# A two-layer cross-attention kernel: layer 2's weight splitting moved into layer 1, with the split tiles kept in DRAM

## The chip, the cores and the metric

The kernel runs on one core of a Trainium2 chip. The metric is the device time of one execution in microseconds (us), the median of the runs listed. Engines are named as the profile does: PE (TensorE), ACT (ScalarE), DVE (VectorE), POOL (GpSimd), and SP (SyncE), whose instruction queue issues nearly all DMAs here.

## What is computed

Two cross-attention layers run one after the other on the same 16 batches of 256 queries (320 channels, 20 heads of 16). The context has 256 rows of 512 numbers. Layer 1 takes 77 rows of it as text and 179 as image tokens, layer 2 takes 252 and 4. Cut to what matters:

```python
def layer(x, ctx, mask, Wq, Wk, Wv, Wk_ip, Wv_ip, Wout, bout):
    text, ip = split(ctx)                       # 77 | 179 rows in layer 1, 252 | 4 in layer 2
    q = x @ Wq; k = text @ Wk; v = text @ Wv
    probs = softmax(q_h @ k_h.T / 4)            # per head
    out = probs @ v_h
    sem = ...                                   # from the text probabilities and the raw context
    ip_probs = softmax(q_h @ (ip @ Wk_ip)_h.T / 4 + 0.5 * sem) * mask
    out = out + ip_probs @ (ip @ Wv_ip)_h
    return out @ Wout + bout + x
```

Everything is float32. The kernel multiplies in a rounded format and keeps accuracy by splitting each operand into a high part and a low part (the remainder) and adding three products.

## The kernel before, in words

Work goes in slots. Layer 1 has 80 (16 batches x 5 groups of four heads, `NS = 80`), layer 2 another 80. `slot0` and `slot1` write the attention of a slot by hand: scores (L744), their maxima (L745, L746 on DVE), the turned scores (L768), exponentials (L771 on ACT), the multiplication by the image factor (L774 on POOL), and the values (L801 on PE), which end in `settle0`. Everything else, such as keys, queries, contexts and the output projection of a finished batch, is a task: a generator with a list of due times in slots. `fill(now)` steps each task whose time has come, between the pieces of a slot. The PE order is exactly the order in which the code is written. On the other engines a scheduler places the instructions, unless `queued` ties one behind the last anchor (the last score maximum, exponential or multiplication) of its engine. Each engine then works through its own list strictly in order, SP's list of DMAs included.

The keys and queries of a slot are loaded by SP four slots ahead (`stacks0`, `LEAD = 4`) into a ring of four tiles each, `ks` and `qs`. Their transfers are `ks<-kd`, `qs<-qd`, `ks<-M` and `qs<-tph`.

The output of a batch b of layer 1 goes through `finish`: `gather` transposes the heads' results (`hT`, L831 on DVE), `split` makes the operand `ho` (L282 on ACT, L283 and L284 on DVE), and `project` multiplies it with `wF` (L609 for two thirds of the rows, L612 for the last). For odd batches the split is due at slot 5b+6 and the first L609 group at 5b+7.2.

Layer 2's weights are prepared late in layer 1 by the tasks `w7` (image keys, then `wA`), `w6` (values `wC`, image values), `w2` (queries `wE`), and in the first slots of layer 2 by `("w4", 1)` (output `wF`). All use `in_turn` and `halves`: a DMA brings a 128-row piece into one of two `rawc` buffers, ACT copies it rounded (L164), and DVE and POOL subtract to get the low part (L167, in three pieces for the weights in heads' layout). Two also multiply a part by a mask (L218). The tiles `wA`, `wC`, `wE` and `wF` hold layer 1's weights until layer 1 is done with them, and `wB` is a ring of four.

Of the kernel before, what the change touches and what calls it, by code (L numbers as in the profile page):

```python
# [8 lines left out]
F32 = mybir.dt.float32  # L9
# [7 lines left out]
B = 16  # L17
S = 256
H = 20
# [31 lines left out]
def xattn2(  # L51
# [129 lines left out]
    def columns(s, m):  # L181

        at = m * 128 if not s else CH + 64 + m * 128
        return slice(at, at + 128)

    def rows(w, k):

        return w[k * 128 : (k + 1) * 128]

    def in_turn(parts, wait, tag="raw", eng=nc.vector, later=False):  # L190

        ahead, parts, tags = [], list(parts), tag.split()
        for i in range(len(parts) + 1):
            if len(tags) > 1:
                new = () if i else range(len(parts))
            else:
                new = range(i + 1 if i else 0, min(i + 2, len(parts)))
            if i:
                halves(*ahead.pop(0), eng, wait)
            for j in new:  # L200
                src, hi, lo = parts[j]
                raw = buf(tags[j // 2 % len(tags)], [128, 512], bufs=2)
                shape = src.shape
                raw = raw[:, : shape[1]] if len(shape) == 2 else raw.rearrange("p (k n) -> p k n", k=shape[1])
# [13 lines left out]
            nc.vector.tensor_scalar_mul(w[:, 2, CH : 2 * CH], f(w[:, 2, CH : 2 * CH]), half)  # L218
        return lambda s, k, m: w[:, k, columns(s, m)]

    def weights_by_column(w_d, wait=0, raw="raw"):

        parts = [buf("wB", [128, 2, 4, 128], FR, bufs=SIZES["WB"]) for m in range(3)]
        src = w_d.rearrange("(k p) n -> p k n", p=128)
        yield from in_turn([(src[:, :, m * 128 : (m + 1) * 128], w[:, 0], w[:, 1]) for m, w in enumerate(parts)], wait, raw)
        return lambda s, k, m: parts[m.start // 128][:, s, k]

    def weights_by_row(w_d, wait=0, raw="raw"):

        parts = [buf("wB", [128, 2 * CH + 4], FR, bufs=SIZES["WB"]) for k in range(4)]  # L230
        yield from in_turn([(rows(w_d, k), *rounded(w)) for k, w in enumerate(parts)], wait, raw)
        return lambda s, k, m: parts[k][:, columns(s, m)]

    def prod(out, lhs, rhs, kt):

# [240 lines left out]

    def weights7():
        cip = w1["cip"]
        wki1 = yield from weights_by_row(wki1_d, 0.3, "rawc")
        for m in range(3):  # L480
            kp = prod_m(bank()[:, :BI], wki1, m, lambda s, k: cip[:, s, k], 4)
            evacuate(kip[:, 0, m], kip[:, 1, m], kp, m)
            yield
        w1["k"] = yield from weights(wk1_d, "wA", None, 0.3, "rawc")

    def weights6():
        cip = w1["cip"]
        wv = w1["wv"] = buf("wC", [128, 2, 4, H * D + NIP], FR)
        parts = [(wv1_d[k * 128 : (k + 1) * 128], wv[:, 0, k, : H * D], wv[:, 1, k, : H * D]) for k in range(4)]
        yield from in_turn(parts, 0.3, "rawc")  # L490
        wvi1 = yield from weights_by_column(wvi1_d, 0.3, "rawc")
        vip = buf("rawc", [128, 512], bufs=2, name="vip")[:BI, :CP]
        for m in range(3):
            ms = slice(m * 128, m * 128 + 128)
            vp = bank()[:BI, :128]
            prod(vp, lambda s, k: cip[:, s, k], lambda s, k: wvi1(s, k, ms), 4)
            nc.vector.tensor_copy(vip[:, ms], vp)
            yield
        ind1 = buf("M", [2, 2, S], FR, bufs=SIZES["M"], name="ind")
        nc.scalar.activation(ind1, ident[:2, :2].unsqueeze(2).to_broadcast([2, 2, S]), AF.Copy, scale=-1.0)  # L500
        w1["ind"] = ind1
        w1["bmask"] = f(buf("kb", [128, CP], FR, name="bmask"))
        dma(w1["bmask"], w1["hop"])
        dma(vipd, vip)
        for i in range(2):
            v = buf("wD", [128, 2, 640], bufs=2, name="v1t")
            nc.gpsimd.memset(v, 0.0)
            nc.vector.memset(vcols(v, V1W)[:, 0, :, 16], 1.0)
            nc.vector.tensor_scalar_add(vcols(v, V1W)[:, 1, :, 16], vcols(v, V1W)[:, 1, :, 16], tmask[:, 2:3])
            v1t.append(v)  # L510
        yield

    def weights2():
        wq.append((yield from weights(wq1_d, "wE", tmask[:, 3:4], 0.3, "rawc")))

    def weights4(l):
        wo.append((yield from weights((wo0_d, wo1_d)[l], "wF", tmask[:, 4:5], (0.1, 0.3)[l], "rawc")))

    def weights3():
        gm = buf("vr", [128, 3 * (H * V0W + 16)], FR, bufs=3, name="gm")  # L520
# [639 lines left out]
    task(("w6",), thirds(13, 67), weights6, ("w7",), *[(x, c) for c in range(B) for x in ("v0", "m0t")])  # L1160
    task(("w2",), [71.6, 72, 72.2, 72.6, 73], weights2, ("q0", B - 1), ("w6",))
# [243 lines left out]
```

## Time and profile before

| what | value |
| --- | --- |
| median of 3 runs | 1512.75 us (1506.99, 1512.75, 1522.51) |
| profiled execution, first to last instruction (its span) | 1510.6 us |
| PE busy / DVE / ACT / POOL | 1433.0 / 1178.0 / 883.7 / 1213.3 us |
| mean granted TensorE clock | 0.976 |
| a period of 10 slots (two batches) in the middle of layer 1 | about 74.5 us |
| a period of 5 slots (one batch) in the middle of layer 2 | about 50 us |

The profiled execution has no time of its own beside its span. It lies 2.15 us under the median. In the profile a row of a group reads: line, engine, operation, tile written <- tiles read, shapes, count | busy us, mean ns | idle time of that engine before it and what ended it. In a table by stretches the columns are busy us of each engine with its number of instructions, then the granted TensorE clock (1.00 is full), the DMA engines' busy share and their GB/s. In the view of waits each row names the instruction that waited, what released it, the total, the number of times and the longest. Layer 1 runs to about 695 us. The stretch from 510 to 720 us, in which layer 1's last batches and layer 2's preparation overlap, is called the turn below.

### The profile page before, as it was taken

The page shows a single profiled execution, that of the slowest core. Times are in us where ns is not written, and L with a number is a line of the kernel's source. Part 1 is how long each engine was busy: PE and PEld are TensorE (multiplying, and loading weights), DVE is VectorE, ACT ScalarE, POOL GpSimd, SP SyncE. Part 2 cuts the span into 40 slices and gives each one's busy share as a digit, 9 for nine tenths or more (in the row PEclk, how much of TensorE's full clock was granted, in tenths as well). Part 3 has the DMA queues.
Part 4 walks back from the last instruction along what each step waited for, and adds up shares of the span by engine and source line. Part 5 has one row for each costly group of instructions (what it writes and reads, how often), then busy time and mean ns, then how long its engine had stood idle before and what let it go on. Part 6 is the DMA issues. An engine that isn't in the chain of part 4 may idle for free.

```text
span 1510.6 us, 36096 instructions
## 1 busy us (share of the span) xinstructions
PE 1433.0 (95%) x12726; PEld 1161.7 (77%) x12726; DVE 1178.0 (78%) x2595; ACT 883.7 (59%) x1973; POOL 1213.3 (80%) x1302
## 2 busy tenths in 40 slices
PE   8789999999999999789999999999999999999996
PEld 7678888888878777576777777777777777777764
DVE  5457777777787788776887888878877887888885
ACT  5346565656555545455665666666666666666561
POOL 4259797979797978886698779887988798879785
PEclk9699999999999999898999999999999999999998
DMA  7867787778777867775434434443444344434311
GB/s 235 200 182 217 205 220 203 221 207 223 201 212 203 226 187 188 171 208 156 124 101 126 126 112 123 130 131 106 124 131 126 109 132 124 123 108 115 101 33 38
DMA packets 231018, 234.38 MB, mean 155 GB/s; under 512 B 39095, under 2 KB 200710, under 8 KB 230822
## 3 DMA queue, kind: packets, MB, share of 16 engines
q1 hardware_dynamic: 228630, 230.77, 55.2%
q8 instruction: 102, 1.67, 0.5%
q10 hardware_dynamic: 2208, 1.30, 0.4%
q14 instruction: 78, 0.64, 0.1%
HBM read 118.04 MB, written 77.10 MB: 129 GB/s over the span
## 4 chain that ended last, share of the span: by engine, by line
PE 76%; DMA 6%; DVE 6%; POOL 5%; issue 3%; ACT 2%; SPq 2%; ACTq 0%; POOLq 0%; DVEq 0%
PE X L939 15%; PE X L239 14%; PE P L801 7%; PE X L609 5%; PE S L744 5%; PE P L951 5%; PE P L961 4%; PE T L768 4%; PE S L897 3%; PE T L891 3%; PE X L612 2%; PE X L249 2%; POOL wt L930 2%; PE X L578 2%; PE X L1064 1%
## 5 line engine op out<-in xcount | busy, mean ns | idle before, releaser
L774 POOL TENSOR_TENSOR P<-P,rs 128x512 f32<-128x512 f32 x320 | 414.0, 1316 | 92.4 <-ACT P L771 91.5
L930 POOL TENSOR_TENSOR wt<-P,ctb 128x512 f32<-128x512 f32 x320 | 410.0, 1305 | 78.2 <-ACT ctb L929 78.2
L939 PE MATMUL X<-ctb,gm 128*128 128x512 f32 x1120 | 306.1, 402 | 5.6 <-DVE wt L940 5.5
L771 ACT ACTIVATE P<-T 128x512 f32<-128x512 f32 x320 | 175.9, 593 | 158.6 <-PE T L768 117.1
L940 DVE TENSOR_TENSOR wt<-X,wt 128x512 f32<-128x512 f32 x320 | 216.2, 680 | 42.7 <-PE X L939 37.3
L939 PEld LDWEIGHTS X<-ctb,gm 128*128 128x128 f32 x1120 | 195.9, 189 | 38.8 <-DVE wt L940 8.2
L911 ACT ACTIVATE P<-T 128x512 f32<-128x512 f32 x320 | 173.1, 593 | 77.9 <-PE T L891 74.6
L929 ACT ACTIVATE ctb<-P 128x512 fp32r<-128x512 f32 x320 | 187.0, 627 | 38.5 <-PE X L939 34.7
L899 DVE TENSOR_REDUCE mn<-S 128x4 fp32r<-128x1008 f32 x160 | 191.3, 1196 | 0.0
L746 DVE TENSOR_REDUCE mn<-S 128x4 fp32r<-128x716 f32 x160 | 142.3, 889 | 0.0
L801 PE MATMUL P<-P,vr 128*32 128x256 f32 x1920 | 127.2, 397 | 2.2 <-DVE tmp L818 2.0
L744 PE MATMUL S<-ks,qs 125*128 125x256 f32 x640 | 118.9, 310 | 7.9 <-DMA ks<-M 3.4
L744 PEld LDWEIGHTS S<-ks,qs 125*128 125x128 f32 x640 | 89.5, 197 | 43.2 <-issue 22.7
L1027 POOL TENSOR_TENSOR r<-u,rs 128x40 f32<-128x40 f32 (+2 forms) x17 | 108.7, 6394 | 3.7 <-DVE u L1024 3.7
L768 PE MATMUL T<-qs,ks 127*128 127x256 f32 x640 | 107.8, 292 | 0.6 <-DMA qs<-mt 0.5
L812 DVE STREAM_TRANSPOSE nt<-P 128x512 f32<-128x512 f32 x80 | 57.0, 712 | 52.9 <-PE P L801 52.4
L745 DVE TENSOR_REDUCE mn<-S 128x4 fp32r<-128x308 f32 x160 | 74.5, 466 | 28.4 <-PE S L744 28.2
L768 PEld LDWEIGHTS T<-qs,ks 127*128 127x128 f32 x640 | 92.2, 198 | 2.0 <-issue 0.9
L801 PEld LDWEIGHTS P<-P,vr 128*32 128x32 f32 x1920 | 57.1, 112 | 43.6 <-issue 5.5
L951 PE MATMUL P<-P,v1t 128*32 128x256 f32 x1280 | 86.5, 388 | 0.0
L609 PE MATMUL X<-ho,wF 128*128 128x256 f32 x512 | 76.0, 291 | 10.3 <-ACT mt L754 4.6
L961 PE MATMUL P<-wt,zone 128*32 128x256 f32 x1280 | 84.8, 379 | 0.3 <-DVE wt L940 0.3
(279 smaller groups left out, 2984.4 us busy)
## 6 DMA issues: line engine op xcount, KB each, us to landing
qd<-q SPq DMA_DIRECT2D x96, 256.0 KB
qs<-tph SPq DMA_DIRECT2D x64, 320.0 KB
rawc<-in_cT_dram SPq DMA_DIRECT2D x60, 256.0 KB
qs<-qd SPq DMA_DIRECT2D x80, 192.0 KB
ks<-kd SPq DMA_DIRECT2D x80, 192.0 KB
ks<-kd SPq DMA_DIRECT2D x160, 96.0 KB
qs<-qd SPq DMA_DIRECT2D x160, 96.0 KB
kd<-kst SPq DMA_DIRECT2D x57, 256.0 KB
```

The costliest lines, as they stand in the source:

```text
L239: last = mm(out, lhs(a, k), rhs(b, k), start=i == 0, stop=i == len(terms) - 1)
L744: mm(sp[:, h], Q[: XROW + T0, h, t * 128 : (t + 1) * 128], K[: XROW + T0, h], start=True, stop=True)
L768: mm(st[p][:, j], K[:KS0, 2 * p + j, t * 128 : (t + 1) * 128], Q[:KS0, 2 * p + j], start=True, stop=True)
L771: exp = anchor(nc.scalar.activation(pt, st[p], AF.Exp, scale=SCALE))
L774: anchor(nc.gpsimd.tensor_mul(pt, pt, rs[:, t : t + 1].to_broadcast([128, 2, S])))
L801: mm(pv[32 * s : 32 * s + 32, o : o + S], v[:, vt, h : h + 32], P[k, s // 2][:, t, s % 2], start=vt < 2, stop=vt != 1,)
L899: anchor(nc.vector.tensor_reduce(maxes[k + 2][:, t], sp[:, :, :T1], axis=AX.X, op=ALU.max))
L911: anchor(nc.scalar.activation(P[k, u][:, t], st[u], AF.Exp, scale=SCALE))
L929: nc.scalar.activation(R[k, u][:, t], P[k, u][:, t], AF.Copy, scale=0.5)
L930: anchor(nc.gpsimd.tensor_sub(W[k, u][:, t], P[k, u][:, t], f(R[k, u][:, t])))
L939: mm(yp, gm[:, gb], R[k, u][:, kt], start=i == 0, stop=i == len(blocks[n]) - 1)
L940: nc.vector.tensor_mul(W[k, u][:, n], yp, W[k, u][:, n])
```

## The change

A new task `pre` (`split_ahead`) runs during layer 1, from slot 8.2 on. It takes the 22 pieces of layer 2's six weights one by one, in three steps each: load into `rawc`; split into a new tile `ws` (one buffer) with the same ACT, DVE and POOL instructions as before, now `queued` behind the anchors; store `ws` to a DRAM tensor in the layout in which it will be used. Five pieces go into each stretch of ten slots, between slots 8 and 15 of it. The tasks `w7`, `w6`, `w2` and `("w4", 1)` then only load finished tiles straight into `wB`, `wA`, `wC`, `wE` and `wF` (`brought`), and their due times are earlier by up to two slots. `w6` loads the image values first and the values after.

```diff
+    WR = 2 * CH + 4
+    ready = {n: dram.tile([k, 128, w], F32, name=f"w{n}") for n, k, w in (("ki", 4, WR), ("k", 4, WR), ("v", 4, 2 * CH), ("vi", 4, 2 * CP), ("q", 3, WR), ("o", 3, WR))}
...
+    def split_ahead():
+        for name, w_d, half in (("ki", wki1_d, None), ("k", wk1_d, None), ("vi", wvi1_d, None), ("v", wv1_d, None), ("q", wq1_d, 3), ("o", wo1_d, 4)):
+            for k in range(w_d.shape[0] // 128):
+                n = CH if name == "o" else w_d.shape[1]
+                raw = buf("rawc", [128, 512], bufs=2)[:, :n]
+                queued(dma(raw, rows(w_d, k)[:, :n]))
+                yield
+                w = buf("ws", [128, 2 * CP], FR)[:, : ready[name].shape[2]]
+                if name in ("v", "vi"):
+                    halves(w[:, :n], w[:, n:], raw, nc.vector, True)
+                else:
+                    halves(*rounded(w, name != "o"), raw, nc.vector, True)
+                    if half is not None and k == 2:
+                        nc.vector.tensor_scalar_mul(w[:, CH : 2 * CH], f(w[:, CH : 2 * CH]), tmask[:, half : half + 1])
+                yield
+                queued(dma(ready[name][k], w))
+                yield
+
+    def brought(name, tag):
+        w = buf(tag, [128, ready[name].shape[0], WR], FR)
+        for k in range(w.shape[1]):
+            queued(dma(w[:, k], ready[name][k]))
+            yield
+        return lambda s, k, m: w[:, k, columns(s, m)]
...
     def weights7():
-        wki1 = yield from weights_by_row(wki1_d, 0.3, "rawc")
+        parts = [buf("wB", [128, WR], FR, bufs=SIZES["WB"]) for k in range(4)]
+        for k, w in enumerate(parts):
+            queued(dma(w, ready["ki"][k]))
...
-        w1["k"] = yield from weights(wk1_d, "wA", None, 0.3, "rawc")
+        w1["k"] = yield from brought("k", "wA")
...
-    task(("w7",), thirds(14, 62), weights7, ("w1",), ("k0", B // 2 - 1))
+    task(("pre",), [8.2 + 10 * (i // 15) + 1.4 * (i // 3 % 5) + (0, 0.9, 1.4)[i % 3] for i in range(66)], split_ahead)
+    task(("w7",), [62.2, 62.6, 63, 63.2, 63.6, 64, 64.2, 64.6, 65], weights7, ("w1",), ("pre",), ("k0", B // 2 - 1))
```

How the instructions then stand, at three places of the second stretch of ten slots. The changed kernel's line numbers are higher: L772 and L773 are L745 and L746 of before, L842 to L845 are L815 to L818, L858 is L831, L276 and L277 are L260 and L261, L298 to L300 are L282 to L284, L166 and L169 are L164 and L167, L798 is L771, L781 is L754.

DVE before, where batch 3's output operand `ho` is made (slot 21). `hT` are the transposed heads, `mn` the score maxima, `X` and `S` PSUM banks:

```order
L831 STREAM_TRANSPOSE hT_1300<-hsn 128x256
L745 TENSOR_REDUCE mn_567<-S 128x4
L746 TENSOR_REDUCE mn_567<-S 128x4
L815 RECIPROCAL P<-nt_136 128x16
L283 TENSOR_TENSOR ho_161<-hT_1300,ho_161 128x512
L284 SCALAR_TENSOR_TENSOR ho_161<-ho_161,tmask,hT_1300 128x256
L816 TENSOR_TENSOR P<-P,mk 128x8
L745 TENSOR_REDUCE mn_566<-S 128x4
L746 TENSOR_REDUCE mn_566<-S 128x4
L818 TENSOR_TENSOR tmp_807<-nt_136,P 128x256
L260 TENSOR_TENSOR X<-X,kst_159 64x2x179
L260 TENSOR_TENSOR X<-X,q_145 64x256
```

DVE after, the same place, from the same reciprocal on:

```order
L842 RECIPROCAL P<-nt_142 128x16
L843 TENSOR_TENSOR P<-P,mk 128x8
L845 TENSOR_TENSOR tmp_813<-nt_142,P 128x256
L858 STREAM_TRANSPOSE hT_1306<-hsn 128x256
L772 TENSOR_REDUCE mn_572<-S 128x4
L773 TENSOR_REDUCE mn_572<-S 128x4
L276 TENSOR_TENSOR X<-X,kst_165 64x2x179
L169 TENSOR_TENSOR ws_1680<-rawc_123,ws_1680 128x260
L276 TENSOR_TENSOR X<-X,q_151 64x256
L277 TENSOR_TENSOR kst_165<-X,both_287 64x2x179
L299 TENSOR_TENSOR ho_167<-hT_1306,ho_167 128x512
L300 SCALAR_TENSOR_TENSOR ho_167<-ho_167,tmask,hT_1306 128x256
```

The low part of a weight piece (L169) has come in, and the two halves of `ho` have moved behind a pair of score maxima and three other subtractions. Of the odd batches, this shift stands at 1, 3, 7, 9 and 13, and not at 5, 11 and 15.

ACT at the same place, before:

```order
L282 CAST ho_161<-hT_1300 128x768
L771 ACTIVATE P_122<-T 128x512
L771 ACTIVATE P_123<-T 128x512
L258 CAST kst_159<-X 64x2x179
L259 COPY both_281<-X 64x358
L258 CAST q_145<-X 64x256
L259 COPY both_280<-X 64x256
L754 CAST mt_222<-X 8x256
```

And ACT after:

```order
L798 ACTIVATE P_128<-T 128x512
L798 ACTIVATE P_129<-T 128x512
L274 CAST kst_165<-X 64x2x179
L275 COPY both_287<-X 64x358
L166 CAST ws_1680<-rawc_123 128x320
L274 CAST q_151<-X 64x256
L275 COPY both_286<-X 64x256
L781 CAST mt_228<-X 8x256
L298 CAST ho_167<-hT_1306 128x768
```

The high part of `ho` has moved from ahead of two exponentials to behind them and five copies, one of which is the weight piece's.

SP before, up to the load of the queries `qs` of slot 23 (`x1d` and `xc` are a finished batch's result and the next residual, `kst` keys on their way out):

```order
L84 DMA xc_116<-in_xT_dram 128x3x256
L84 DMA kd_70<-kst_159 128x2x512
L84 DMA kd_70<-kst_159 128x512
L84 DMA qs_98<-tph_263 80x4x256
L84 DMA ks_102<-M_260 80x4x179
L84 DMA ks_102<-kd_70 48x4x256
L84 DMA qs_98<-qd_1734 48x1024
```

SP after, the same stretch:

```order
L84 DMA x1d<-xc_122 128x3x256
L84 DMA xc_122<-in_xT_dram 128x3x256
L84 DMA kd_70<-kst_165 128x2x512
L84 DMA kd_70<-kst_165 128x512
L84 DMA ks_108<-kd_70 48x4x256
L84 DMA rawc_124<-in_wk_dram 128x384
L84 DMA qs_104<-tph_269 80x4x256
L84 DMA ks_108<-M_266 80x4x179
L84 DMA wk<-ws_1680 128x644
L84 DMA qs_104<-qd_1748 48x1024
```

A load and a store of a weight piece have come between the keys and the queries of slot 23, and the batch's result, which was sent off four loads earlier, now stands at the head of this stretch.

More of the change, by code (lines that the diff above doesn't have):

```diff
@@ L219, in weights @@
         return lambda s, k, m: w[:, k, columns(s, m)]
[L221 to L232, printed above, removed]
+    def split_ahead():
[21 more added lines that the diff above has]
+        return lambda s, k, m: w[:, k, columns(s, m)]
     def prod(out, lhs, rhs, kt):
@@ L478, in weights7 @@
         cip = w1["cip"]
[L479 removed]
+        parts = [buf("wB", [128, WR], FR, bufs=SIZES["WB"]) for k in range(4)]
+        for k, w in enumerate(parts):
+            queued(dma(w, ready["ki"][k]))
+            if k % 2:
+                yield
         for m in range(3):
[L481 removed]
+            kp = prod_m(bank()[:, :BI], lambda s, k, m: parts[k][:, columns(s, m)], m, lambda s, k: cip[:, s, k], 4)
             evacuate(kip[:, 0, m], kip[:, 1, m], kp, m)
             yield
[L484 removed]
+        w1["k"] = yield from brought("k", "wA")
     def weights6():
         cip = w1["cip"]
+        parts = [buf("wB", [128, 2, 4, 128], FR, bufs=SIZES["WB"]) for m in range(3)]
+        for m, w in enumerate(parts):
+            for s in range(2):
+                at = slice(s * CP + m * 128, s * CP + m * 128 + 128)
+                queued(dma(w[:, s], ready["vi"][:, :, at].rearrange("k p n -> p k n")))
+            yield
+        for c in range(B):
+            get("v0", c), get("m0t", c)
         wv = w1["wv"] = buf("wC", [128, 2, 4, H * D + NIP], FR)
[L489 to L491 removed]
+        for s in range(2):
+            queued(dma(wv[:, s, :, :CH], ready["v"][:, :, s * CH : (s + 1) * CH].rearrange("k p n -> p k n")))
+            yield
         vip = buf("rawc", [128, 512], bufs=2, name="vip")[:BI, :CP]
[L493 to L494 removed]
+        for m, w in enumerate(parts):
             vp = bank()[:BI, :128]
[L496 to L497 removed]
+            prod(vp, lambda s, k: cip[:, s, k], lambda s, k: w[:, s, k], 4)
+            nc.vector.tensor_copy(vip[:, m * 128 : (m + 1) * 128], vp)
             yield
@@ L513, in weights2 @@
     def weights2():
-        wq.append((yield from weights(wq1_d, "wE", tmask[:, 3:4], 0.3, "rawc")))
+        wq.append((yield from brought("q", "wE")))
     def weights4(l):
-        wo.append((yield from weights((wo0_d, wo1_d)[l], "wF", tmask[:, 4:5], (0.1, 0.3)[l], "rawc")))
+        wo.append((yield from brought("o", "wF") if l else weights(wo0_d, "wF", tmask[:, 4:5], 0.1, "rawc")))
     def weights3():
```

4 lines of the change are left out of this document (2 added, 2 removed).

## The prediction

> **What bounds the kernel now.** The page's first part and its clock row come first: which engine is busy all the time, and where it is not.
>
> ```profile
> span 1510.6 us, 36096 instructions
> PE 1433.0 (95%) x12726; PEld 1161.7 (77%) x12726; DVE 1178.0 (78%) x2595; ACT 883.7 (59%) x1973; POOL 1213.3 (80%) x1302
> PEclk9699999999999999898999999999999999999998
> ```
>
> PE is busy 95% of the span, so time is won only where PE waits or runs at a lower clock. The clock row dips at slices 16 and 18 (a slice is 37.8 us, so from 604 to 718 us): the turn. The table by stretches then compares the middle of both layers with the turn.
>
> ```profile
> 284.00:359.00 75.00, 73.93 (x706) 63.95 (x709) 58.44 (x139) 44.23 (x104) 66.23 (x65) 1.00 0.77 215
> 860.00:960.00 100.00, 99.08 (x884) 77.48 (x883) 83.07 (x178) 63.91 (x138) 84.11 (x92) 1.00 0.45 122
> 440.00:450.00 10.00, 8.43 (x80) 7.31 (x84) 8.44 (x20) 5.61 (x14) 7.12 (x9) 1.00 0.82 225
> 560.00:570.00 10.00, 10.00 (x82) 9.20 (x82) 5.51 (x15) 5.15 (x16) 6.56 (x10) 0.84 0.52 134
> 600.00:610.00 10.00, 7.02 (x77) 4.94 (x69) 9.87 (x22) 5.81 (x16) 7.26 (x9) 1.00 0.82 201
> 610.00:620.00 10.00, 8.22 (x71) 6.51 (x72) 6.25 (x16) 4.61 (x10) 5.73 (x8) 0.66 0.84 198
> 640.00:650.00 10.00, 8.09 (x66) 6.07 (x65) 8.03 (x16) 5.03 (x11) 10.00 (x12) 0.83 0.81 200
> ```
>
> In the middle of layer 1 PE is busy 73.93 of 75 us at full clock, in layer 2 99.08 of 100. Nothing is to be won there, and each us that a change makes PE wait there is lost. In the turn PE falls to 7.02 of 10 us while DVE stands at 9.87. Who makes it wait there tells the view of PE's waits from 540 to 660 us, and how much of DVE's work is weights the groups of the same stretch:
>
> ```profile
> PE X L685 <- ACT sp L681: 3.5, 1, 3.5
> PE X L752 <- DVE mn L746: 2.2, 3, 0.8
> PE X L609 <- DVE wE L218: 1.9, 1, 1.9
> PE X L666 <- DVE xc L847: 1.7, 1, 1.7
> PE X L666 <- DVE q L261: 0.7, 1, 0.7
> PE X L239 <- DVE wB L167: 0.6, 1, 0.6
> PE X L239 <- ACT wB L164: 0.4, 1, 0.4
> ACT wB L164 <- DMA rawc<-in_wvi_dram: 2.2, 2, 1.7
> L167 DVE TENSOR_TENSOR wC<-rawc,wC 128x320 fp32r<-128x320 f32 x4 | 4.8, 1200 | 0.0
> L167 DVE TENSOR_TENSOR wB<-rawc,wB 128x260 fp32r<-128x260 f32 x4 | 2.9, 744 | 0.6 <-ACT wB L164 0.6
> L167 DVE TENSOR_TENSOR wA<-rawc,wA 128x260 fp32r<-128x260 f32 x4 | 2.7, 682 | 1.1 <-ACT wA L164 0.9
> L167 DVE TENSOR_TENSOR wB<-rawc,wB 128x512 fp32r<-128x512 f32 x3 | 2.6, 880 | 0.6 <-ACT wB L164 0.6
> L218 DVE TENSOR_SCALAR wE<-wE,tmask 128x320 fp32r<-128x320 f32 x1 | 1.5, 1490 | 0.0
> ```
>
> **What the turn gains.** The five DVE groups sum to 14.5 us, taken off DVE in a stretch where it is full. Waits of PE that end on weight work: 1.0 us on the image keys' tiles (0.6 + 0.4), 1.9 on the masked `wE`, and 3.5 on the softmax copy L681. That copy is put down to itself, but ACT stood ahead of it at a weight cast that waited for its load (the L164 row, longest 1.7 us). The 2.4 us of L666 (1.7 + 0.7) stand behind two `wC` subtractions, in the stretch from 590 to 600 us. Together 8.8 us. Of the 2.2 us of L752 I count half, since DVE serves other work as well: 9.9 us. Then the clock: 10 us at 0.84, 0.66 and 0.83 are 1.6, 3.4 and 1.7 us of lost PE work, 6.7 in all, each behind one of those waits. I take 5 of it, so 15 us. The bounds: 7 us if half of the waits merely pass to the next thing in DVE's list and half of the clock loss stays, 20 us if all goes.
>
> The loads that take the place of the splitting (19 in the turn and 3 later) run on SP ahead of queries and keys of slots 66 to 75. In that stretch no row above has PE waiting for a DMA. I cost them at 0; they are covered by the loads' lead of several slots, and if that cover is gone each costs the time of its own transfer, about 1.2 us for 322 KB at the 279 GB/s that 215 GB/s at a share of 0.77 come to.
>
> **What layer 1 pays, first part: the split itself.** Per ten slots five pieces: five ACT casts, five to fifteen subtractions. DVE has 16.6 us of 75 free and ACT 30.8, so the work fits by its amount. The order does not let it fit by its place. These rows of the timeline (start, length, instruction, in brackets the engine's idle time before it) show how batch 3's output operand meets PE before:
>
> ```profile
> 235.45 0.24 DVE L815 RECIPROCAL P<-nt 128x16 f32<-128x16 f32 x1
> 235.61 0.67 DVE L283 TENSOR_TENSOR ho<-hT,ho 128x512 fp32r<-128x512 f32 x1
> 236.20 1.52 DVE L284 SCALAR_TENSOR_TENSOR ho<-ho,tmask,hT 128x256 fp32r<-128x256 f32 x1
> 236.27 0.69 PE L744 MATMUL S<-ks,qs 125*128 125x256 f32 x4
> 237.71 0.46 DVE L745 TENSOR_REDUCE mn<-S 128x4 fp32r<-128x308 f32 x1
> 237.82 0.36 ACT L754 CAST mt<-X 8x256 fp32r<-8x256 f32 x1
> 238.10 0.89 DVE L746 TENSOR_REDUCE mn<-S 128x4 fp32r<-128x716 f32 x1
> 238.24 1.22 PE L609 MATMUL X<-ho,wF 128*128 128x256 f32 x8 [0.80 <-ACT mt L754]
> 239.24 0.52 DVE L260 TENSOR_TENSOR X<-X,kst 64x358 f32<-64x358 f32 x1
> 239.68 0.41 DVE L260 TENSOR_TENSOR X<-X,q 64x256 f32<-64x256 f32 x1
> 240.01 0.51 DVE L261 TENSOR_TENSOR kst<-X,both 64x358 fp32r<-64x358 f32 x1
> ```
>
> L609 starts at 238.24, half a us after L284 ends (237.72), and PE had already waited 0.80 us there. By the order after, DVE does after the reciprocal: L816, L818 and the transpose (about 1 us, to 236.7), then the pair of maxima, which needs PE's scores of 236.27 to 236.96 and takes 1.28 us from first start to last end (237.71 to 238.99), so to 238.25; then L260 0.52, the weight piece 0.7 (rows of `wA` and `wB`), L260 0.41, L261 0.51, L283 0.67, L284 1.52: 4.3 us, to 242.6. Instructions that follow each other overlap by some 0.07 us in these rows, which takes 0.5 off: 242.1. The last two of the eight L609 matmuls need it, so the group ends near 242.3 and not at 239.46 (238.24 + 1.22): 2.8 us later, and 2.0 if L284 takes half as long, 3.4 without the overlap. PE's order is unchanged, so the whole of PE stands behind it. This shift is there at batches 1, 3, 7 and 9 inside layer 1. The other odd places look alike in the waits of PE from 110 to 508 us:
>
> ```profile
> PE X L609 <- ACT mt L754: 4.0, 5, 0.8
> PE X L239 <- DVE sp L669: 2.5, 1, 2.5
> ```
>
> Five waits of 0.8 us, so there is no slack at any of them. Four times 2.8 us: 11 us. Both ends: 0 if the scheduler's order leaves room that I don't see, 4 x 3.4 = 14.
>
> **Second part: the DMAs.** Ten more per ten slots, 5 x 192 KB in and 5 x 322 KB out, 2.6 MB; at 279 GB/s 9.4 us of the 17 us that the share of 0.77 leaves free in 75. Where they go in front of a load they can delay it. Slot 23's queries:
>
> ```profile
> 223.87 0.71 SPq L84 DMA_DIRECT2D qs<-qd  x1
> 230.17 0.69 PE L744 MATMUL S<-ks,qs 125*128 125x256 f32 x4
> ```
>
> 6.3 us from issue to use, and 514 KB more in front (1.9 us). PE's waits from 110 to 508 us name no DMA, so the load has landed by then with an unknown rest. Per ten slots two such places: 0 to 2 x 1.9 us over five stretches, 0 to 19 us. I take 2, near the lower end, since 6.3 us is more than three times the addition. The store also makes SP wait until POOL has done the piece; behind it stand just these loads, so this wait is in the same bounds. POOL's own two short subtractions per piece (0.6 us) are hidden: POOL is busy 66.23 of 75 us.
>
> **The sum.** -15 + 11 + 2 = -2 us against the span of 1510.6. The runs' median lies 2.15 us above that, so 1512.75 - 2, about 1511 us.
>
> **The rivals.** A, the loss in layer 1 does not come (0 to 4 us instead of 13), because DVE gets to `ho` sooner than I count: DVE and ACT have free time in the middle of layer 1. Against it stands the 0.80 us wait of the quoted row. With a gain of 15 to 20 it gives 1493 (1512.75 - 20) to 1502 (1512.75 - 15 + 4), in the middle 1497.
>
> B, slower, by the clock. Two single long waits of PE:
>
> ```profile
> 441.57 1.25 PE L239 MATMUL X<-cta,wB 128*128 128x360 f32 x6 [2.48 <-DVE sp L669]
> 611.78 0.49 PE L685 MATMUL X<-ident,sp 128*77 128x128 f32 x1 [3.50 <-ACT sp L681]
> ```
>
> The one of 3.5 us lies in the stretch with 0.66 over 10 us, 3.4 us lost; the one of 2.5 us lies in the stretch from 440 to 450 us, whose clock stayed at 1.00. The point of decision thus lies between 2.5 and 3.5 us of idle PE. At batch 3 PE would idle 0.8 + 2.8 us, cut into pieces by the L609 matmuls that need only the high part. If each of the four waits tips it, they cost 4 x (2.8 + 3.4) = 25 us: -15 + 25 + 2 = +12, or +20 with a gain of 7 in the turn, 1525 to 1533; with late queries up to 1545. [...]
>
> C, the change does not free the turn: DVE's and POOL's other work keeps PE waiting, the gain is 7 us or less. Then -7 + 13 = +6, 1519. The 2.2 us of L752 speak for it, the 8.8 us of waits on weights against.
>
> **How the numbers follow.** Forecast and C, where gain and loss nearly cancel: 0.46 (0.35 and 0.11). A: 0.28. B: 0.26. The range that holds 8 in 10 reaches into A and B: 1490 to 1537. The likeliest case's own range is 1501 (gain 20, loss 8) to 1523 (gain 7, loss 17). Faster by over 1% is under 1497.6, slower by over 1% over 1527.9; 1% is about what a measurement of this kernel can tell from no change. Of A about 0.2 lies under the first; of B 0.22 over the second, and of C 0.02 with it: faster 0.2, within 0.56, slower 0.24.
>
> **What would show it.** In the changed kernel's profile: from 540 to 660 us no L167 group from `rawc` into `wA`, `wB` or `wC`, PE's waits there down by 9 us, the clock near 1.00 up to 650 us; the turn's slots about 15 us shorter. In layer 1 four waits of PE at the output projection (L609's line) of 2 to 3.5 us, put down to DVE's second half of `ho`, and the ten-slot stretches with them longer than 74.5 us by 2.8; the stretch of batch 5 not. A clock under 1.00 behind them would be B. No such waits would be A, and then my reading of the order is wrong. Waits for `qs<-qd` would show that I set the DMAs too low.

## The result, and the profile after

The changed kernel takes 1556.15 us (median of 4 runs, 1551.72 to 1570.78), the kernel before 1514.86 us on the same chip: a ratio of 1.0316, with a 95% interval of 1.0276 to 1.0355. It is slower, by 42 to 54 us on the 1512.75 us shown before. The profiled execution has a span of 1568.9 us and so lies at the upper end of its runs, as run 3's below does; the sums below go by ratios of medians, the profile is used for places and causes.

From the first part of the page and its clock row, after:

```profile
span 1568.9 us, 36123 instructions
PE 1464.3 (93%) x12726; PEld 1175.1 (75%) x12726; DVE 1187.6 (76%) x2596; ACT 884.3 (56%) x1974; POOL 1213.0 (77%) x1302
PEclk9699898999999999989999999999999999999998
```

The busy times of DVE, ACT and POOL hardly changed: the work was moved, not added. PE fell from 95 to 93% of a longer span, and the clock row (a digit is tenths of full speed, 9 is 0.9 or more) now also dips in slices 4 and 6, counted from 0 as in the prediction (a slice is 39.2 us, so from 157 to 196 and from 235 to 274 us), inside layer 1, where before it stood at 9 throughout. The table by stretches shows the middle of layer 1 (450 us) before and then after, with PE busy first and the clock third from the end:

```profile
110.00:560.00 450.00, 436.24 (x4145) 376.87 (x4145) 353.74 (x816) 262.34 (x619) 391.23 (x379) 1.00 0.77 211
110.00:560.00 450.00, 414.44 (x3699) 349.83 (x3688) 333.49 (x736) 241.78 (x570) 357.38 (x359) 0.94 0.74 211
```

In the same 450 us PE is idle 22 us more (436.24 - 414.44), and it is granted 0.94 of the clock while it runs, which is another 25 us (0.06 of 414.44). So the loss stands in layer 1, half of it as waits and half as clock. Layer 2 runs at the old pace: five of its slots in the middle take 49.9 to 50.0 us in both kernels. Who makes PE wait in layer 1, from 110 to 570 us:

```profile
PE X L779 <- DVE kst L169: 12.6, 4, 4.4
PE X L636 <- DVE ho L299: 4.2, 4, 2.0
PE X L636 <- ACT mt L781: 4.1, 4, 1.2
PE S L771 <- DVE mn L773: 4.1, 1, 4.1
PE T L795 <- DMA qs<-mt: 2.8, 2, 2.0
```

The waits at L636 (L609 before) for the low part of `ho` (L299 and L300) are those that I forecast. The largest row, L779, I had not: PE's transpose of the maxima needs a bank of PSUM that DVE's subtraction for the keys (`kst`) has still to read. The timeline shows what DVE does in that time (first SP's queue and ACT's queue, then ACT, DVE and PE):

```profile
148.73 1.40 SPq L84 DMA_DIRECT2D wki<-ws  x1
151.38 1.69 ACTq L783 DMA_DIRECT2D qs<-mt  x2
153.18 1.08 ACT L798 ACTIVATE P<-T 128x512 f32<-128x512 f32 x2 [3.34 <-PE X L265]
154.77 0.46 ACT L166 CAST ws<-rawc 128x320 fp32r<-128x320 f32 x1 [0.51 <-DMA wki<-ws]
155.26 1.36 DVE L169 TENSOR_TENSOR ws<-rawc,ws 128x260 fp32r<-128x260 f32 x1 [2.78 <-ACT ws L166]
157.08 0.52 DVE L169 TENSOR_TENSOR kst<-X,kst 128x358 fp32r<-128x358 f32 x1
157.66 0.38 PE L779 MATMUL X<-ident_r,mn 128*8 128x128 f32 x2 [3.85 <-DVE kst L169]
```

Read from the bottom: PE waits 3.85 us for `kst`; `kst` stands behind the piece's subtraction in DVE's order; DVE idles 2.78 us there until ACT has cast the piece. ACT's cast comes last behind the store of the piece before, because the pieces share one tile, `ws`, but that is only 0.51 us of it. Most of the rest is ACT's pair of exponentials, which ends at 154.26; ahead of it ACT stood idle for 3.34 us, up to the end of two issues of `qs<-mt`, the small transfers of the maxima; what holds those stands below, under runs 9 to 12. All four waits at L779 have such late exponentials (ACT idle for 2.3 to 3.4 us ahead of them), and two of the four a wait for the store (0.51 and 2.48 us). No wait of PE names a store.

### The profile page after: what moved, and what is told of

It reads as the page before. It is cut to its first block, busy times and chain, and to the rows that moved or that the text cites. A ratio compares the mean times of both kernels' runs of the same rounds, so it can differ in the third digit from the quotient of the medians.

```text
span 1568.9 us, 36123 instructions
## 1 busy us (share of the span) xinstructions
PE 1464.3 (93%) x12726; PEld 1175.1 (75%) x12726; DVE 1187.6 (76%) x2596; ACT 884.3 (56%) x1974; POOL 1213.0 (77%) x1302
## 4 chain that ended last, share of the span: by engine, by line
PE 67%; DMA 10%; DVE 7%; POOL 6%; issue 4%; ACT 3%; SPq 2%; ACTq 0%; DVEq 0%; POOLq 0%
PE X L966 15%; PE X L255 11%; PE P L828 6%; PE X L636 5%; PE P L978 5%; PE P L988 4%; PE S L771 4%; PE T L918 3%; PE S L924 3%; PE T L795 3%; POOL P L801 3%; DMA qs<-mt 2%; SPq L84 2%; PE X L639 2%; PE X L605 2%
## 5 line engine op out<-in xcount | busy, mean ns | idle before, releaser
L798 ACT ACTIVATE P<-T 128x512 f32<-128x512 f32 x320 | 176.3, 593 | 211.8 <-PE T L795 154.8
L773 DVE TENSOR_REDUCE mn<-S 128x4 fp32r<-128x716 f32 x160 | 142.4, 890 | 0.0
L828 PE MATMUL P<-P,vr 128*32 128x256 f32 x1920 | 139.3, 424 | 1.7 <-POOL P L801 1.3
L771 PE MATMUL S<-ks,qs 125*128 125x256 f32 x640 | 121.2, 314 | 11.3 <-DVE mn L773 5.5
L771 PEld LDWEIGHTS S<-ks,qs 125*128 125x128 f32 x640 | 91.4, 201 | 49.3 <-issue 29.8
L795 PE MATMUL T<-qs,ks 127*128 127x256 f32 x640 | 113.3, 298 | 11.5 <-DMA qs<-mt 8.7
L772 DVE TENSOR_REDUCE mn<-S 128x4 fp32r<-128x308 f32 x160 | 74.8, 467 | 34.0 <-PE S L771 33.2
L636 PE MATMUL X<-ho,wF 128*128 128x256 f32 x512 | 82.4, 304 | 16.4 <-DVE ho L299 5.3
L636 PEld LDWEIGHTS X<-ho,wF 128*128 128x128 f32 x512 | 72.6, 204 | 27.2 <-DVE ho L299 6.7
```

Source lines behind the costliest of these rows:

```text
L636: mm(pp, w(s, k, m), a[:, t], start=i == 0, stop=i == len(terms) - 1)
L771: mm(sp[:, h], Q[: XROW + T0, h, t * 128 : (t + 1) * 128], K[: XROW + T0, h], start=True, stop=True)
L795: mm(st[p][:, j], K[:KS0, 2 * p + j, t * 128 : (t + 1) * 128], Q[:KS0, 2 * p + j], start=True, stop=True)
L798: exp = anchor(nc.scalar.activation(pt, st[p], AF.Exp, scale=SCALE))
L828: mm(pv[32 * s : 32 * s + 32, o : o + S], v[:, vt, h : h + 32], P[k, s // 2][:, t, s % 2], start=vt < 2, stop=vt != 1,)
```

## The experiments

All ratios are to the kernel before, measured beside each; the intervals reach 0.002 to 0.006 to either side (3 to 9 us).

**1. A second staging tile.** Is it the one `ws`?

```
-                w = buf("ws", [128, 2 * CP], FR)[:, : ready[name].shape[2]]
+                w = buf("ws", [128, 2 * CP], FR) if k % 2 or name == "vi" else buf("wt", [128, WR], FR)
+                w = w[:, : ready[name].shape[2]]
```

> The changed kernel with a second staging tile: pieces alternate between `ws` and a new tile `wt`, except the four of the image values' weights, which stay on `ws` alone (slots 24 to 31 are thus a control). Buffer theory (ACT's cast of a piece waits until the store of the piece before has landed, and DVE, in order, stands behind that cast with a bank of PSUM that PE wants): DVE's waits for the cast fall from 13.3 us to the control's share of 4 or less, PE's waits at the maxima's transpose from 12.6 to under 5 us, and the time falls by 20 to 35 us to 1520 to 1536. Order theory (the stalls come from what DVE does ahead of the second half of `ho`, with or without a wait): no more than 5 us less, 1550 or over. Transfer theory (the stores and loads themselves slow queries, keys and maxima): the same time as the changed kernel, since the bytes are the same.

1548.24 us, ratio 1.0236 (1.0189 to 1.0283). DVE's waits for the cast of a piece only fell from 13.3 to 10.4 us, PE's at the transpose from 12.6 to 8.8. The second tile is worth some 12 us (0.008 of 1512.75; 3 to 21 by the two intervals), about a quarter of the loss. The buffer theory as a whole falls: most of the time stays.

**2. Layer 1's part alone.** The kernel before, with the split added as dead work (the function, the tile list and the task of the change, nothing else).

> The kernel before, with the split during layer 1 added as dead work: the 22 pieces are loaded, split and stored as in the changed kernel, and nobody reads them; the turn splits its weights again as before. It gives the price of layer 1's part alone. If the loss of 41 us lies in layer 1 (buffer, order and transfer theories alike) and the turn gives nothing back, the time is the changed kernel's, 1550 to 1560. If the turn gains what I predicted (15 us) the time is 15 us over the changed kernel's, about 1571. If the loss lies in the turn's loads, it is under 1530.

1547.3 us, ratio 1.0234 (1.0192 to 1.0275): 35 us, most of the loss, comes without any change in the turn. It is 12 us less than the whole change costs (4 to 21 by the two intervals), so the changed turn gains nothing on top of it.

**3. The turn's part alone.** One piece split and stored, all tiles loaded from it.

```
-        for name, w_d, half in (("ki", wki1_d, None), ...
-            for k in range(w_d.shape[0] // 128):
+        for name, w_d, half in (("vi", wvi1_d, None),):
+            for k in range(1):
...
+    ready = {n: one[:, :w].unsqueeze(0).to_broadcast([k, 128, w]) for n, k, w in ...
```

> The changed kernel with one piece split and stored in place of 22; all tiles of layer 2's weights are loaded from that one piece with the same shapes and at the same places (it leaves out the split of the other 21 pieces; layer 2 computes with wrong weights). It gives the turn's part alone. If the turn gains as I predicted: 1515 - 15 = 1500, bounds 1495 to 1508. If the loads' late arrivals and the clock eat the gain, as the slots 60 to 79 of the changed kernel read (5 us longer than before): 1515 to 1520. If the turn's loss was only layer 1's delay carried over: under 1500.

1510.82 us, ratio 1.0011 (0.9983 to 1.0040): no gain. The table by stretches, the turn before and in this kernel:

```profile
525.00:690.00 165.00, 144.58 (x1299) 118.86 (x1297) 130.73 (x277) 85.11 (x199) 130.31 (x149) 0.93 0.69 181
525.00:690.00 165.00, 143.73 (x1258) 115.23 (x1258) 115.33 (x264) 77.22 (x181) 123.14 (x128) 0.94 0.76 210
```

DVE (third) did lose its 15 us, 130.73 to 115.33, and PE (first) got none of it: 144.58 and 143.73, at the same clock, with a DMA share of 0.76 in place of 0.69. PE's waits there have changed their names, from 525 to 705 us:

```profile
PE T L796 <- DMA qs<-mt: 2.9, 4, 1.7
PE X L780 <- DVE mn L774: 2.7, 4, 0.8
PE X L256 <- DMA wB<-one: 2.3, 2, 1.3
PE S L772 <- DMA qs<-mt: 1.8, 1, 1.8
```

Rows of maxima (`qs<-mt`) and the finished tiles themselves now arrive last.

**4. No stores in layer 1.** All loads and the whole split stay, one store of 22 is left.

> The changed kernel with its loads and its split, but only one of the 22 stores; layer 2's tiles are all loaded from that one piece (it leaves out 21 stores; layer 2 computes with wrong weights). Buffer theory: no cast waits for a landing any more, DVE's waits for the cast nearly go, and the time is 20 to 35 us under the changed kernel's, 1520 to 1536, close to the run with two staging tiles. Order theory: DVE's work and its order are the same, 1545 to 1556. Transfer theory: half of the bytes are gone, so about half of the loss, 1530 to 1540, with DVE's waits for the cast still there.

1543.11 us, ratio 1.0211 (1.0164 to 1.0258). The stores with all that waits for them are worth 16 us (1.0316 - 1.0211; 7 to 25 by the intervals), and 32 us stay without them. PE's waits at the transpose fell to 5.8 us, those at the output projection stayed.

**5. DVE relieved.** The pieces' subtractions on POOL.

```
-                    halves(*rounded(w, name != "o"), raw, nc.vector, True)
+                    halves(*rounded(w, name != "o"), raw, nc.gpsimd, True)
```

> The changed kernel with every subtraction (and the masking) of the pieces on POOL in place of DVE; ACT's casts, the loads, the stores and the single staging tile stay. DVE has no piece left to wait for or to do. By DVE's order, `ho` still stands two maxima later at the odd batches inside layer 1. If what costs is DVE's standing at a piece ahead of the keys' subtraction (PE's waits of 12.6 us at the maxima's transpose), those waits go and the time falls by 12.6 us and as much again of clock, to 1525 to 1535. If it is the later `ho` alone, they go but the time stays over 1540. If POOL, in its own order, becomes the engine that PE waits for, PE's waits name POOL and the time is 1556 or over.

1573.53 us, ratio 1.0424 (1.0381 to 1.0466), the slowest of all. PE's waits for `ho` grew (15.3 us for its cast on ACT, five places). Those at the transpose for `kst` did not go: 10.5 us in four places, against 12.6. So `kst` comes late without any piece on DVE. DVE now waits for the keys' cast on ACT itself (3.2 to 3.8 us at three of the four), and ACT's list is late as before: its exponentials come after 2.7 to 3.8 us of idle time, its cast of the piece after 1.4 to 1.7 us of waiting for the store.

**6. Other places.** Two tiles and another row of times. With it a context takes the raw tile of some pieces before they are split, so part of layer 2's weights is wrong; instructions and bytes are the same.

```
-[8.2 + 10 * (i // 15) + 1.4 * (i // 3 % 5) + (0, 0.9, 1.4)[i % 3] for i in range(66)]
+[11.7 + 10 * (i // 15) + 0.8 * (i // 3 % 5) + (0, 0.9, 1.4)[i % 3] for i in range(66)]
```

> The changed kernel with two staging tiles (as in the first run) and another row of times: pieces of a pair of batches start at 11.7, 12.5, 13.3, 14.1 and 14.9 of every ten slots in place of 8.2, 9.6, 11, 12.4 and 13.8. By DVE's order no piece then stands ahead of the keys' subtraction of the odd slots, and `ho` is moved at batches 3 and 9 only, no longer at 1 and 7. Order theory: PE's waits at the maxima's transpose under 3 us in layer 1, waits at the output projection at batches 3 and 9 alone, the time 1520 to 1530. Amount theory (DVE, ACT and the transfers are slowed by the work as such, wherever it stands): 1545 to 1550, as with two staging tiles.

1540.63 us, ratio 1.0205 (1.0164 to 1.0247): 10 us over the upper end of what the order theory expected, and 5 us under the first run by the ratios, which is within their intervals. The waits at the transpose for `kst` are gone, as that theory had it, and others came: 3.5 us at the scores for `mn` and 2.4 at the outputs for `tmp` (single ones of 1.2 to 1.3 us between the old places, where nothing waited before), 4.7 at the keys' products for `sp`. A piece put elsewhere found another victim there. On `ho` itself the run is a control: the five slots around the places of batches 3 and 9, where it still moves `ho`, take 40.9 us each, those of batches 1 and 7, where it does not, 37.5 and 38.7 (37.4 before).

**7. The turn with 5 loads in place of 19**, on the base of the third run (and 1 in place of the 3 after it).

> The turn alone, as in the run of the third kernel, with 5 loads of ready tiles in the turn in place of 19 (one for each of the five weights; the rest of each tile isn't filled and the products read the one loaded part; it leaves out the split and most loads, and layer 2 computes with wrong weights). If the loads, which I priced at nothing, are what ate the gain of 15 us: PE's waits for the rows of maxima and for `wB` (8.0 us in the turn of the third run) go, and the time is 1495 to 1503. If the gain was never there, since what stood behind the weights' work waits for the next thing in the order: 1508 to 1515, as in the third run, with waits for other work in their place.

1503.11 us, ratio 0.9967 (0.9945 to 0.9989): a gain of 5 us, 2 to 8. So the loads that I costed at nothing cost 7 us (1.0011 - 0.9967; 1 to 12 by the intervals), and with few of them the gain is still 5 and not 15: PE's waits from 525 to 690 us now name other work.

```profile
PE X L784 <- DVE mn L778: 3.6, 5, 1.1
PE X L641 <- ACT ho L300: 2.1, 1, 2.1
PE S L776 <- DMA kb<-hop: 1.9, 1, 1.9
```

**8. Without the second and the third of every five pieces' split**, loads and stores kept.

> The changed kernel without cast and subtractions of the second and the third of every five pieces (9 of 22; their loads and stores stay; it leaves out that part of the split and layer 2 computes with partly wrong weights). These two stand ahead of the keys' subtraction and of `ho`. By DVE's order `ho` stays moved at batches 1 and 3 and isn't moved at 7 and 9: a control inside the run. Order theory: PE's waits at the maxima's transpose under 3 us, waits of some 2 us at the output projection at batches 1 and 3 only, slots 40 to 44 and 50 to 54 as in the kernel before, the time 1515 to 1528. Amount theory: 13 of 22 pieces, so 13/22 of 41 us, 1537.

1541.7 us, ratio 1.0216 (1.0175 to 1.0258): a loss of 33 us, 26 to 39. That is far over the order theory's figure (1515 to 1528) and still over the amount theory's (a loss of 24), so neither fits. The control inside it speaks for the order at the output projection all the same: at batch 1, where `ho` is still moved, PE waits there 2.3 us (1.2, 0.6 and 0.5); at batches 7 and 9, where it isn't, 0.8 us each, as before. Much of the rest sits at the transpose (4.9 us for `kst`, and 1.9 us each put down to the stores `wk<-ws` and `wo<-ws`, which this run keeps).

**9 to 12. The loss split by kind.** Neither theory alone had fitted, so the last four take one kind each: all transfers without the split (of 20 of the 22 pieces, here and in the last two); the split without transfers (on a tile that is always there); that without ACT's casts; that with casts only.

```
# 9                 if k == 0 and name in ("ki", "vi"):
#                       ... the split ...
# 10, 11, 12
-                raw = buf("rawc", [128, 512], bufs=2)[:, :n]
-                queued(dma(raw, rows(w_d, k)[:, :n]))
+                raw = held[:, :n]
```

> The changed kernel with all 22 loads and 22 stores of the pieces and no cast and no subtraction for 20 of them (it leaves out that work; layer 2 computes with wrong weights). The level to compare with is the turn alone, 1511. The two runs before showed that moving the pieces or leaving out two of five brings little, so the loss is now split by kind. Transfer theory (the pieces' loads and stores delay queries, maxima and the casts of others): 1525 to 1535. Work theory (ACT's and DVE's instructions cost, wherever they stand): 1511 to 1518.

> The changed kernel with casts and subtractions of all 22 pieces, each on one tile that is always there, with no loads of pieces and one store (it leaves out the transfers; layer 2 computes with wrong weights). `ho` is moved at batches 1, 3, 7 and 9, as in the changed kernel. Work theory: the loss is here without any transfer, 1530 to 1543 against 1511 for the turn alone. Transfer theory: 1511 to 1520.

> As the run with work only, without ACT's casts for 20 of the 22 pieces: DVE and POOL subtract at once and wait for nobody (it leaves out casts and transfers). `ho` is moved at the same batches. If DVE's standing at a piece until ACT has cast it is what costs: 1511 to 1520, with the waits at the moved `ho` left, about 8 us. If DVE's own added instructions cost: the same as the run with work only, 1530 to 1543.

> As the run with work only, with ACT's 22 casts and no subtractions for 20 of the 22 pieces (it leaves out subtractions and transfers). `ho` is moved at batch 1 only. If DVE's part costs (its order, its work or its wait): 1511 to 1516, with a wait of 2 us at the output projection of batch 1 only. If ACT's order costs (maxima rows and exponentials behind the casts): 1520 or over.

Transfers only: 1531.11 us, ratio 1.0129 (1.0080 to 1.0179). Work only: 1533.21, 1.0141 (1.0086 to 1.0196). Work without casts: 1534.69, 1.0146 (1.0091 to 1.0201). Casts only: 1517.72, 1.0044 (1.0012 to 1.0076). So both kinds cost about the same, and of the work it is the subtractions, with or without a wait for ACT: without transfers, DVE's standing at a cast costs nothing that can be seen.

Work only is the cleanest look at what I had forecast. PE's waits from 110 to 570 us in it:

```profile
PE X L639 <- ACT mt L784: 6.0, 6, 1.2
PE X L258 <- DVE sp L699: 4.8, 3, 2.4
PE X L639 <- DVE ho L302: 3.5, 4, 1.1
PE X L639 <- DVE ho L303: 2.2, 4, 0.6
```

The four waits for `ho` L302 are at batches 1, 3, 7 and 9, three of those for L303 at 1, 3 and 7 (the fourth, 0.6 us, at batch 11, at the edge of the turn), and no wait for `kst` is left. The table by stretches at batches 9 and 7, and at batch 5, whose `ho` is not moved:

```profile
480.00:490.00 10.00, 9.49 (x63) 7.13 (x63) 6.25 (x12) 2.06 (x5) 4.96 (x4) 0.66 0.40 104
400.00:410.00 10.00, 8.46 (x56) 6.00 (x57) 6.60 (x13) 2.18 (x5) 4.87 (x4) 0.66 0.35 89
320.00:330.00 10.00, 9.45 (x86) 8.21 (x86) 10.00 (x19) 6.44 (x14) 8.43 (x8) 1.00 0.64 172
```

At these two moved places the clock is 0.66 over 10 us, so PE loses 3.2 and 2.9 us besides its waits; behind batch 1 it is 0.84 over 10 us, behind batch 3 0.92 and 0.91 over two such stretches, about half of that loss; at batch 5 it is 1.00. The five slots around the moved places (from the starts of the slots' score matmuls) take 41.4, 41.2, 42.8 and 41.7 us against 37.4 before; those around batch 5 take 37.6. Four places, 17.5 us.

Transfers only shows the other half. Four small transfers of 2 KB each bring a slot's maxima into the operand. ACT issues them one after the other and does its exponentials behind them. At batch 1:

```profile
149.51 4.20 ACTq L784 DMA_DIRECT2D qs<-mt  x2
153.81 1.09 ACT L799 ACTIVATE P<-T 128x512 f32<-128x512 f32 x2 [6.69 <-PE X L637]
154.78 0.47 ACT L166 CAST kst<-X 128x358 fp32r<-128x358 f32 x1
155.28 0.53 DVE L169 TENSOR_TENSOR kst<-X,kst 128x358 fp32r<-128x358 f32 x1 [4.22 <-ACT kst L166]
155.87 0.29 PE L780 MATMUL X<-ident_r,mn 128*8 128x128 f32 x2 [2.67 <-DVE kst L169]
```

The last two of the four issues stand 3.6 us apart (149.51 and 153.14), while a piece's load and store (192 and 322 KB) and the loads of keys and queries are under way. ACT stands idle for 6.69 us before its exponentials, the keys' cast comes behind them, `kst` behind that, and PE waits 2.67 us, put down to DVE. From the first issue of a slot's four to the last it takes 2.49 us in the mean of layer 1 before, 3.14 in the changed kernel and 3.09 in run 9; over 4.2 us in 1 of 55 slots before, in 9 of 47 in the changed kernel and in 5 of 51 in run 9.

The changed kernel's trace names the semaphore that a DMA's issue waits for and the one on which its landing events are counted. ACT's and SP's DMAs share eight semaphores there, 230 or 231 issues on each. At the same batch 1 the last two of the four (in the row at 151.38 of the section on the result) each wait for the one on which they report. The first, at 151.38, comes 0.02 us after the last landing event (151.36) of SP's `ks<-kd`, issued at 145.32 on the same semaphore. The second, at 152.50, comes 0.02 us after the last one (152.48) of a piece's load, `rawc<-in_wki`, issued at 146.67. So 2 KB wait for the landing of two transfers of 192 KB with which they have nothing to do but the semaphore. From 110 to 515 us, issues of `qs<-mt` that start so, with ACT idle ahead of them, are 12 before (6.0 us of idle time in all), 13 in run 10 (8.9), 32 in run 9 (29.8) and 21 in the changed kernel (17.5): with the added transfers ACT is held more often and longer. What the rows would win with semaphores of their own, no run has tried.

**The account**, in us on 1512.75, by ratios: the turn +1.7 (run 3); the work 19.7 (run 10 less run 3); the loads 10.6 (run 4 less run 10); the stores 15.9 (the change less run 4); together 47.8, which they must be, since each run is taken from the next. Each figure but the turn's (4 us to either side) has 9 to 11 us to either side, so the loads alone are not clear of nothing; loads and stores together, 26.5, are. Counted apart, work 19.7 and transfers 17.8 (run 9 less run 3) make 37.5. The 9 us left over would be the price of having both at once, and the 12 that the second tile brings would fit it, but with 13 us to either side that is not shown.

## Why the prediction was wrong

**What bounds the kernel.** Right: PE sets the time, in layer 1 each wait of PE is lost, and layer 2 did not change.

**The turn, -15 (bounds 7 to 20).** Wrong twice. The step "I cost them at 0; they are covered by the loads' lead of several slots" failed: 19 loads cost 7 us. What I looked at was the tile that a load brings. What came late besides (PE's 4.7 us for `qs<-mt` in run 3) were the small rows of maxima of the attention, whose issues wait for semaphores that SP's transfers hold: from 525 to 705 us 4 were held so before (3.1 us), 11 in run 3 (7.6) and 7 in run 7 (5.0). PE's waits before did not name this in the stretch that I looked at, but ACT's did in layer 1, from 110 to 515 us:

```profile
ACT P L771 <- DMA qs<-mt: 9.5, 4, 2.8
```

The price that I named for lost cover, 1.2 us a load, was over twice what was measured (7 us for 16 loads fewer, 14 of them in the turn, so under 0.5 each), but it was nearer than the nothing that went into the sum. And the gain without the loads was 5 us, under my lower bound of 7: taking 15 us off a full DVE let it reach its next item sooner, and PE then waited for maxima, `ho` and `kb` instead. I subtracted waits by the name of their last releaser; in an order fixed for all engines, most had a second one close behind.

**Layer 1, the order of `ho`, +11.** Right in mechanism and in place: batches 1, 3, 7 and 9, not 5, and gone at 7 and 9 when `ho` is put back (run 8). The waits are smaller than forecast: in run 10 about 2.5 us at a place, (4 x 1.2 + 3.5 + 1.6) / 4, so 1.7 more than the 0.8 of before, where I had counted 2.8 more. The price is larger, 4.4 us (17.5 / 4), since the clock drops behind each. That was rival B's price, and its point of decision was what I got wrong: "between 2.5 and 3.5 us of idle PE" in one piece. Here two or three waits of 0.4 to 1.2 us within 4 us were enough, and in run 3 single waits of 2.4 to 2.5 us were, where one of 2.48 us before was not; the last section has the counts. Taken as a bound on one single wait, as I took it, that point is contradicted by the runs: these drops come at waits of at most 1.2 us.

**The transfers, +2 (bounds 0 to 19).** The mechanism was half right, the size at the end of its bounds and over: 18 us by themselves, 27 on top of the split (9 and 10 us to either side). I looked for the delay at the load of the queries, which SP issues; it came at the rows of maxima, which ACT issues with its own work queued behind, and which wait for the landing of SP's transfers. I took the value near the lower end because PE's waits named no DMA. They hardly name one after either: in run 9 the chain ends in `DVE kst`. And of the store I wrote that SP waits for POOL there; that the next piece's cast must wait until the store has landed, since there is one `ws`, I didn't write down at all. It stands in the diff: a tile without a count of buffers, read by a transfer.

**The rivals.** B (1525 to 1545) was on the right side, with the clock as it came, and too short by the transfers. A fell with run 10. C's "the change does not free the turn" came true, in part for the reason given (other work keeps PE waiting: 5 us in run 7, under C's 7), in part by the loads, which C left out. The range ended at 1537, inside B: the one case that let the transfers and the clock both go wrong, B's upper end of 1545, lay outside it and was still 11 us short.

**What stays open.** Why run 6, with the old waits gone, still loses 31 us was followed only to the names of the new waits. The whole change costs 12 us more than run 2, though its turn alone costs 1.7: the 10.7 us left are a little more than the three intervals allow (9.7). In the profiled executions, one of each kernel, most of it lies in the turn: slots 60 to 79 take 173.4 us before, 166.7 in run 2, 174.6 in run 3 and 182.8 in the changed kernel. Why the turn costs more behind the whole split was not traced.

## What to carry to other kernels

Before work is moved into a stretch where PE is busy 97% of the time, ask for each piece which instruction stands behind it on its engine, who waits for that one, and what happens if the piece is late: free engine time by amount (16.6 of 75 us on DVE here) did not hide the work, which cost 19.7 us in the fixed order. A transfer is not free because PE's waits name no transfer: look for the small ones that an engine issues between its own instructions, and for the semaphore that each issue waits for (2 KB rows here, behind 17.5 us of ACT's idle time in the changed kernel). And ask whether a staging tile that is stored has as many buffers as pieces can be under way: with one, ACT's cast waited up to 2.48 us for a store, and a second was worth some 12 us.

## What the hardware showed

**Where the granted clock fell to half.** The trace records the granted clock. In the changed kernel, from 110 to 510 us, the stretches at 0.50 begin at 156.79, 170.44, 214.81, 248.95, 262.60, 289.91, 341.11, 419.61, 433.26 and 491.29 us, which are 4, 13, 10, 4, 8, 15, 23, 4 and 17 steps of 3.413 us apart, and last one or two steps. In the kernel before, those from 559.71 to 703.07 us stand 15, 6, 4, 4, 6 and 7 such steps apart. Counted in such steps over both traces, from 60 to 1500 us: of the 758 steps at full clock in which PE has no matmul for less than 1.2 us, 1 is followed by half clock; of the 22 with 1.7 us or more, all 22; of the 16 between, 5. So in these two traces the drop goes with the sum of the idle time inside one step, and with where a wait falls on the grid. In run 3 the stretches of 10 us around three single waits at L256, of 2.4 to 2.5 us (the row of four has 8.6 in all), have a clock of 0.83. The wait of 2.48 us that ends at 441.57 us before is cut by the grid at 440.24, into 1.15 and 1.33 us, and the clock stays at 1.00. In the changed kernel around batch 3 three stretches of 10 us read:

```profile
240.00:250.00 10.00, 5.58 (x40) 5.29 (x41) 4.69 (x13) 3.30 (x9) 5.24 (x8) 0.95 0.93 262
250.00:260.00 10.00, 9.62 (x67) 7.43 (x65) 5.38 (x12) 4.83 (x11) 6.23 (x8) 0.71 0.64 207
260.00:270.00 10.00, 6.79 (x41) 4.36 (x42) 6.84 (x11) 2.19 (x6) 3.44 (x5) 0.66 0.39 106
```

The stretch after a wait of 4.4 us (to 249.31) runs at 0.71 though PE is busy 9.62 of 10 us; the next has waits of 1.6 and 2.0 us and runs at 0.66. In run 10 a place costs 4.4 us where its waits grew by 1.7.

**A DVE instruction that lasted as long as a series of POOL's.** The first half of `ho` on DVE (L283) takes 0.67 us at batch 3 before and 1.66 at batch 2; at batch 2 in the changed kernel (L299) it takes 5.88 us; the rows of DVE, then of POOL:

```profile
207.88 5.88 DVE L299 TENSOR_TENSOR ho<-hT,ho 128x512 fp32r<-128x512 f32 x1 [1.35 <-ACT ho L298]
213.68 0.47 DVE L300 SCALAR_TENSOR_TENSOR ho<-ho,tmask,hT 128x256 fp32r<-128x256 f32 x1
207.82 1.29 POOL L169 TENSOR_TENSOR cta<-rawc,cta 128x512 fp32r<-128x512 f32 x1
209.07 0.46 POOL L846 TENSOR_TENSOR hsn<-tmp 128x128 f32<-128x128 f32 x1
209.49 1.27 POOL L169 TENSOR_TENSOR cta<-rawc,cta 128x512 fp32r<-128x512 f32 x1
210.73 2.48 POOL L801 TENSOR_TENSOR P<-P,rs 128x512 f32<-128x512 f32 x2
```

POOL runs without a gap from 207.82 to 213.21, and DVE's instruction, begun at 207.88, ends half a us later, at 213.76; PE's single wait of 4.1 us at L771 follows from it. That the one held the other is my reading of the two rows; no run varied it. The kernel before has such a place too: there a masked subtraction into `hq` takes 3.67 us at 437.69, under POOL's series of 434.45 to 441.08, and the wait of 2.48 us at 441.57 that the prediction quotes stands behind it; the five slots from slot 47, which hold it, take 39.9 us, those from 17, 27 and 37 37.1. The two profiles do not have all such places in common (batch 2's 5.88 us against 1.66), so places of single profiles are compared above only where a cause was seen.
